# A decoder layer with routed experts: an earlier split of the routing, another order of its last logits and exponentials, and eight instead of six token tiles projected among the expert products

## The chip, the cores and the metric

The kernel runs on one core of one Trainium2 chip. The metric is the time of the whole program on the device in microseconds (us); lower is better. The engines' names are those of the profile: PE is TensorE (matrix products; PEld is its loading of weights), DVE is VectorE, ACT is ScalarE, POOL is GpSimd and SP is SyncE, which only issues DMAs in this kernel. "SPq" in a profile line is SP's DMA queue.

## The reference

One decoder layer on 16 sequences of 100 tokens, 512 wide, in float32. The part around the change is the last third:

```python
x = layernorm(x + self_attention(x))
x = layernorm(x + cross_attention(x, ctx, mask))      # ends with out @ Wo, out 2048 wide
# feed-forward: two of eight experts for each token
logits   = x @ router_w + router_b
top, idx = top_k(logits, 2)
weight   = softmax(top)
h        = silu(x @ expert_w[e] + expert_b[e])         # the reference does this for every expert e
combined = sum of weight * h[idx]
y        = x + combined @ proj_w + proj_b
x        = layernorm(x + norm_w * y / sqrt(mean(y*y) + 1e-6))
```

The kernel computes only the two chosen experts of each token.

## The kernel before

The 1600 tokens are 13 tiles of 128 (NT = 13; the last has 64). Every float32 product is made of three matmuls on PE: each operand is split (`split`, L139 to L142) into a high part, rounded to the fp32r type, and a low part, the rest, and `mm3` (L147 to L149) adds high x high, low x high and high x low. A tile of 128 x 512 times a 512 x 512 matrix is therefore 4 x 3 = 12 matmuls.

The work around the change, in its order:

1. *The output product of the cross-attention and its layer norm* (`d_part`, `d_norm`; PSUM bank `acc`; the operand halves are `ot_h`, `ot_l`). Tile after tile, each in four groups of heads; the last three tiles (TAIL = 3: 10, 11, 12) are interleaved group by group. Among them the expert weights are loaded and split into WH and WL.
2. *Router.* `d_turn(t)` transposes tile t (L985, bank `ptx`) and copies it to `x2f` (L992); `d_logits(t)` makes its 8 logits (L1004, L1008). `choose(a, b)` (L1110) takes the two largest logits of tiles a to b on DVE and ranks the tokens of each expert by small matmuls (L1149, L1160, bank `gb`).
3. *Slots.* Tokens are gathered by expert into NSL = 32 slots of 128 rows. This is done twice. `settle(0, CUT)` places the tokens of the first CUT tiles, and `slots(0, EARLY, CUT)` makes by index matmuls (L1314) the row lists of the first EARLY slots, so that these can be gathered before the last tiles are normed. `settle(CUT, NT)` and `slots(EARLY, NSL, NT)` do the rest when all tiles are routed. settle is some 40 small DVE instructions.
4. *Expert products.* For each slot i: `e_gather` (POOL, indirect DMA of rows into `xs`), `e_turn` (PE transposes into `pte`, split into `xsT`), `e_bias` (SP loads the expert's bias row `eb`), `e_product` (12 matmuls into `ph_i`), `e_out` (DVE adds the bias into `h`, L1381; ACT makes Silu of it, L1382; SP stores it to `ysd`, L1383). `h` has two buffers, `eb` three.
5. *Projection and the last norms* of a token tile: `f_gather` (POOL fetches its two rows y from ysd), `f_load` (z, which is x plus the projection's bias, and x), `f_sum` (weighted sum of the two rows), `f_turn` (transposes, bank `ptc`), `f_split`, `f_product` (12 matmuls into `pp`), then `f_square`, `f_mean`, `f_first`, `f_second` (the sums of squares, the roots, the two norms, the store of the output `out<-z`, L1694). REST tiles do this among the expert products, at the slots that the list TURN names; the rest follow after the last expert product. Tiles from LATE = 9 on gather their rows after all stores to ysd.

The weights of the two chosen experts come from the two largest logits: `ex = exp(top1 - top0)` (L1482, L1483), then 1/(1+ex). exp and Silu need different tables on ACT, so each change between them issues an ACT_TABLE_LOAD.

Each engine runs its own queue in order. Which order that is a scheduler decides when the program is built; it orders the recorded instructions by dependences and priorities: `tc.high_priority` lifts a block, `in_turn(a, b)` puts a behind b, and `tc.keep_in_program_order` fixes a DMA's place. PSUM banks are taken by name: `mm`, `s`, `t`, `av` have two each, and a bank is free for its next user when the last reader has read it. DMA issues of the hardware queues go round over eight completion counters.

Of the kernel before, what the change touches and what calls it, by code (L numbers as in the profile page):

```python
# [9 lines left out]
FP = mybir.dt.float32  # L10
FR = mybir.dt.float32r
AF = mybir.ActivationFunctionType
ALU = mybir.AluOpType
# [4 lines left out]
B, S, D = 16, 100, 512  # L18
T = B * S
KC = D // 128  # L20
# [43 lines left out]
def tile_decoder_layer(  # L64
# [29 lines left out]
    nc = tc.nc  # L94
# [3 lines left out]
    def pool(stack, name, bufs=1, **k):  # L98
        return stack.enter_context(
            tc.tile_pool(name=name, bufs=bufs, reuse_waits="tile", **k)  # L100
        )
# [6 lines left out]
    def bank(tag, shape, name):  # L108
        return ps[-1].tile(shape, FP, name=name, tag=tag)
# [12 lines left out]
    def in_turn(ins, prev):  # L122

        if prev is not None:
            tc.add_manual_dep(
                ins.ins,
                prev.ins.name,
                mybir.DependencyInfo(
                    mybir.DependencyClass.NoSync, mybir.DependencyReason.DATA
                ),  # L130
                reason="in_turn",
            )
        return ins
# [11 lines left out]
    def mm3(out, a, b, start, stop):  # L145

        nc.tensor.matmul(out, a.h, b.h, start=start, stop=False)  # L147
        nc.tensor.matmul(out, a.h, b.l, start=False, stop=False)  # L148
        nc.tensor.matmul(out, a.l, b.h, start=False, stop=stop)  # L149
# [64 lines left out]
    def kp(w):  # L214
        return w.rearrange("(k p) n -> p k n", p=128)

    NT = len(TT)
# [8 lines left out]
    w1 = pool(a_l, "a_1", 1)  # L226
# [347 lines left out]
    for k in range(KC):  # L574
        i = 4 * NU - 8 + k
# [40 lines left out]
    w1 = pool(b_l, "b_1", 1)  # L616
# [113 lines left out]
    w1 = pool(c_l, "c_1", 1, side="right")  # L730
# [134 lines left out]
    TAIL = 3  # L865
# [95 lines left out]
    gw = pool(gs, "gate", side="right")  # L961
    d_l = ExitStack()
    w1 = pool(d_l, "d_1", 1, side="right")
# [14 lines left out]
    XT2, PL = {}, {}  # L978

    def d_turn(t):  # L980
        t0, n = TT[t]
        x2 = X2.pop(t)
        pt = bank("t", [128, KC, 128], f"ptx2_{t}")
        for k in range(KC):
            nc.tensor.transpose(  # L985
                pt[:, k, :n], x2[:n, k * 128 : (k + 1) * 128], ident[:n, :n]
            )
        if t < NT - 1:
            XT2[t] = w1.tile([128, KC, 128], FP, name=f"x2f_{t}", tag="x2f")
        else:  # L990
            XT2[t] = raw[:, 0].rearrange("p (k n) -> p k n", n=128)
        nc.scalar.copy(XT2[t][:, :, :n], pt[:, :, :n])  # L992
        nc.gpsimd.tensor_tensor(x2[:n], x2[:n], pb[:n], ALU.add)
        nc.sync.dma_start(xbd[t][:n], x2[:n])
# [21 lines left out]
    URGENT = 1000  # L1016
    I32, HF = mybir.dt.int32, mybir.dt.float16
    NSL = NE + (2 * T - NE) // 128
    CUT, EARLY = NT - 4, 11

    assert EARLY <= 2 * CUT - (NE - 1)

# [39 lines left out]
    top = gw.tile([128, 2, NT], FP, name="top")  # L1062
# [243 lines left out]
    def slots(a, b, upto):  # L1306

        m = b - a
        todo = [(j, t) for t in range(upto) for j in range(2)]
        o1, o2 = 512 - 2 * m, 512 - m  # L1310
        inv, who = gb[:, o1:o2], gb[0:1, o2:]
        for dst, of in ((inv, named), (who, opens.unsqueeze(3))):
            for i, (j, t) in enumerate(todo):
                nc.tensor.matmul(  # L1314
                    dst,
                    of[:, j, t, :],
                    is_in[:, j, t, a:b],
                    start=(i == 0),
                    stop=(i == len(todo) - 1),
                )  # L1320
        idx = k1.tile([128, m], I32, name=f"idx_{a}")
        nc.vector.tensor_copy(idx, inv)
        wat = k1.tile([1, m], I32, name=f"wat_{a}")
        nc.vector.tensor_scalar(wat, who, float(KC * D), None, ALU.mult)
        bat = k1.tile([1, m], I32, name=f"bat_{a}")
        nc.vector.tensor_scalar(bat, who, float(D), None, ALU.mult)
        for i in range(a, b):
            at_ = slice(i - a, i - a + 1)
            SLOT[i] = idx[:, at_], wat[:, at_], bat[:, at_]
# [30 lines left out]
    def e_product(i, among={}):  # L1360
        xT = XS.pop(i)
        r = nc.tensor.value_load(SLOT[i][1], min_val=0, max_val=(NE - 1) * KC * D)
        ph = bank("mm", [128, D], f"ph_{i}")
        for k in range(KC):
            mm3(ph, xT[:, k, :], ew[:, bass.ds(r + k * D, D)], k == 0, k == KC - 1)
            if k in among:
                among[k]()
        PH[i] = ph

    EB = {}  # L1370
    acted = [None]

    def e_bias(i):
        rv = nc.sync.value_load(SLOT[i][2], min_val=0, max_val=(NE - 1) * D)
        EB[i] = ebb.tile([128, D], FP, name=f"eb_{i}", tag="eb", bufs=3)
        nc.sync.dma_start(EB[i], expert_b[bass.ds(rv, D)].partition_broadcast(128))

    def e_out(i):
        ph = PH.pop(i)
        h = ebb.tile([128, D], FP, name=f"h_{i}", tag="h", bufs=2)  # L1380
        nc.vector.tensor_tensor(h, ph, EB.pop(i), ALU.add)  # L1381
        acted[0] = nc.scalar.activation(h, h, AF.Silu)  # L1382
        nc.sync.dma_start(ysd[i * 128 : (i + 1) * 128, :], h)  # L1383

    early = [1, 2, 4, 5]
# [17 lines left out]
    for i in range(HEAD * NKV, len(parts)):  # L1403
        t, g = parts[i]
        if i + 1 < len(parts):
            d_load(i + 1)
        among = {}
        if t < NT - TAIL:
            if g == 1:
                d_turn(t - 1)  # L1410
            if g == 3:
                among = d_logits(t - 1)
            if g == 0 and t in (2, 4, 6, 8):
                load_expert(early[t // 2 - 1])
        elif t > NT - TAIL and g == 0:
            if t < NT - 1:
                d_turn(NT - TAIL - 1)
            else:
                among = d_logits(NT - TAIL - 1)
        elif (t, g) == (NT - 1, NKV - 1):  # L1420
            d_turn(NT - TAIL)
        d_part(i, among)
        if g == NKV - 1:
            with tc.high_priority(offset=URGENT if t >= NT - TAIL else 0):
                d_norm(t)
        if t == NT - 1 and g < NKV - 1:
            load_expert(wo_slot[g])
        if (t, g) == (CUT, 0):
            nc.sync.dma_start(raw, kp(expert_w[wo_slot[3]])[:, 2:])
        if t % 3 == 0 and t <= CUT and g == 3:  # L1430
            choose(t - 3, t)
        if (t, g) == (NT - 1, 0):
            choose(CUT, CUT + 1)
        if (t, g) == (CUT, 3):
            settle(0, CUT)
            slots(0, EARLY, CUT)
        if (t, g) == (NT - 1, 1):
            for k in range(4):
                e_gather(k)
# [11 lines left out]
    def at_once(t):  # L1451
        with tc.high_priority(offset=URGENT):
            for f in d_logits(t).values():
                f()

    e_product(1, {1: lambda: at_once(NT - 1)})
    e_turn(3)
    e_product(2, {0: lambda: at_once(NT - 2)})
    d_l.close()
    e_l = ExitStack()  # L1460
    ebb = pool(e_l, "ebb")
    for i in range(TAIL):
        e_bias(i)
    for i in range(TAIL):
        e_out(i)
    with tc.high_priority(offset=URGENT):
        choose(CUT + 1, NT)
        settle(CUT, NT)
        slots(EARLY, NSL, NT)
    slot_f = gw.tile([128, 2 * NT], FP, name="slot_f")  # L1470
    nc.vector.scalar_tensor_tensor(
        slot_f,
# [5 lines left out]
    )  # L1478
    slot = k1.tile([128, 2, NT], I32, name="slot")
    nc.vector.tensor_copy(slot.rearrange("p j t -> p (j t)"), slot_f)  # L1480
    ex = gw.tile([128, NT], FP, name="ex")
    nc.vector.tensor_tensor(ex, top[:, 1, :], top[:, 0, :], ALU.subtract)  # L1482
    nc.scalar.activation(ex, ex, AF.Exp)  # L1483
    g1 = k1.tile([128, NT], FP, name="g1")
    nc.vector.tensor_scalar(g1, ex, 1.0, None, ALU.add)
    nc.vector.reciprocal(g1, g1)
# [24 lines left out]
    F, L, C = {}, {}, {}  # L1511


    REST, LATE = 6, 9

    TURN = (19, 20, 22, 23, 25, 26, 28, 29, 31)
    BEHIND = 2

    def upto(t):
# [44 lines left out]
    def f_sum(t):  # L1564
        n = TT[t][1]
        c, y1 = F[t][0]
        ins = nc.scalar.activation(c[:n], c[:n], AF.Copy, scale=g1[:n, t : t + 1])
        tc.keep_in_program_order(in_turn(ins, acted[0]))
        nc.vector.scalar_tensor_tensor(
            c[:n], y1[:n], g2[:n, t : t + 1], c[:n], ALU.mult, ALU.add  # L1570
        )
# [45 lines left out]
    def f_mean(t):  # L1617
# [7 lines left out]
    steps = [([t, t + 1], [t - 2, t - 1] if t else []) for t in range(0, REST, 2)]  # L1625
    FIRST = len(steps)
    steps += [
        ([6], [4, 5]),
        ([7, 8], [6]),
        ([9, 10], [7, 8]),  # L1630
        ([11], [9, 10]),
        ([12], [11]),
        ([], [12]),
# [131 lines left out]
    for t in range(LATE):  # L1765
        assert TURN[t] >= upto(t)
        for lag, f in enumerate((f_fetch, f_prepare, f_project)):
            if t < REST or lag < 2:
                due.setdefault(min(TURN[t] + lag, NSL), []).append((lag, f, t))
    for i in range(FIRST):  # L1770
        due.setdefault(TURN[2 * i + 1] + 3, []).append((3, f_norm, i))
    e_bias(TAIL)
# [15 lines left out]
    for t in range(LATE, NT):  # L1788
        f_gather(t)
    done = FIRST  # L1790
    for t in range(REST + 1, LATE):
        f_load(t)
    for k in range(REST, NT + 3):
        if LATE <= k + 2 < NT:
# [90 lines left out]
```

## Time and profile before

| what | value |
|---|---|
| three runs | 1406.97, 1410.84, 1412.98 us; median 1410.84 |
| the profiled execution | 1408.13 us; span of the trace 1406.4 us |
| granted PE clock, mean over the span | 0.976 of full speed |
| busy share of the span | PE 95%, DVE 67%, ACT 54%, POOL 51% |
| output product of the cross-attention ends | 1205.4 us |
| first slots' settle on DVE | 1171 to 1198 us |
| second ranking, second settle and index matmuls | 1236.3 to 1251.2 us |
| last expert product ends | 1355.4 us |
| projections still to make after it | 8 of 13 tiles |
| last projection's last matmul ends | about 1393 us |

Times are counted from the span's start. A profile line has the start, the busy time of one entry, the engine, the source line, the operation, `out<-in` by the program's names, the shape, and in brackets how long the engine had been idle and what released it. "x3" means that three like instructions are shown as one entry. A stretch's line has its bounds, its length, and the busy time of each engine in it.

PE is the busy engine over the whole, and it runs at nearly the full clock. A full-speed matmul starts 0.23 us after the one before, at the halved clock 0.427 us.

### The profile page before, as it was taken

To read this page: it belongs to the slowest core of one execution; us is meant where nothing else is said; L and a number is where in the kernel's file an instruction comes from. 1 tells how busy PE (TensorE), PEld (TensorE's weight loads), DVE (VectorE), ACT (ScalarE), POOL (GpSimd) and SP (SyncE) were. 2 spreads that over 40 slices of the span, in tenths; PEclk is the share of its full clock that TensorE was granted. 3 is DMA by queue.
4 is the path that set the end of the run, shared out by engine and by line. 5 is a ranking of instruction groups with operands and counts; after the bars stand their busy time and mean duration, and the time that the engine had idled before them with its cause. 6 is when DMAs were issued, how large, how long until landed. Compare 5 with 4: busy or idle time off the path is not lost.

```text
span 1406.4 us, 25135 instructions
## 1 busy us (share of the span) xinstructions
PE 1331.6 (95%) x7928; PEld 1105.0 (79%) x7928; DVE 942.8 (67%) x2933; ACT 756.4 (54%) x1897; POOL 710.3 (51%) x840
## 2 busy tenths in 40 slices
PE   8999989999999999999999999999999898899894
PEld 7888868888778888888888888878887676677773
DVE  5776677776467777777777767767654558754576
ACT  4666643444446666666666666656654233333356
POOL 6878753344245555555555555545455444532530
PEclk9999989999999999999999999999999999899997
DMA  5221363544442122322233312322446545667883
GB/s 170 68 74 58 124 194 96 131 92 114 100 94 72 42 70 71 76 78 70 71 76 78 74 46 67 73 68 51 118 101 182 178 167 164 211 214 240 256 252 118
DMA packets 199160, 161.74 MB, mean 115 GB/s; under 512 B 133581, under 2 KB 153265, under 8 KB 199029
## 3 DMA queue, kind: packets, MB, share of 16 engines
q1 hardware_dynamic: 189191, 139.77, 36.2%
q0 software_dynamic: 4576, 14.95, 3.4%
q10 hardware_dynamic: 5262, 5.41, 1.3%
q8 instruction: 65, 1.06, 0.3%
q14 instruction: 66, 0.54, 0.1%
HBM read 107.25 MB, written 50.99 MB: 113 GB/s over the span
## 4 chain that ended last, share of the span: by engine, by line
PE 68%; DVE 14%; DMA 7%; ACT 4%; issue 3%; POOL 1%; SPq 1%; ACTq 1%; DVEq 0%; POOLq 0%
PE pq L147 4%; PE pq L148 4%; PE pq L149 4%; PE pv L147 4%; PE pv L148 4%; PE pv L149 4%; PE ptp L819 3%; PE pk L147 3%; PE pk L149 3%; PE pk L148 3%; PE s L147 3%; PE s L148 3%; PE s L149 3%; PE av L148 2%; PE av L147 2%
## 5 line engine op out<-in xcount | busy, mean ns | idle before, releaser
L811 POOL TENSOR_SCALAR p<-p,sums 100x361 f32<-100x361 f32 x256 | 146.4, 577 | 99.4 <-DVE sums L810 88.2
L798 DVE CUSTOM_DVE_ANT_0 p<-s,nmask 100x361 f32<-100x361 f32 x256 | 133.0, 527 | 63.4 <-PE s L149 54.7
L809 ACT ACTIVATE p<-p,nm 100x361 f32<-100x361 f32 x256 | 153.2, 601 | 39.6 <-DVE nm L798 36.3
L142 DVE TENSOR_TENSOR pT_l<-ptp,pT_h 128x400 fp32r<-128x400 f32 (+1 forms) x192 | 107.5, 568 | 57.2 <-ACT pT_h L139 56.8
L147 PE MATMUL pq<-WH 128*128 128x512 f32 (+2 forms) x272 | 107.2, 394 | 5.3 <-DVE WH L141 5.3
L819 PE MATMUL ptp<-ident,p 100*128 100x100 f32 (+1 forms) x768 | 107.4, 252 | 0.0
L139 ACT CAST pT_h<-ptp 128x400 fp32r<-128x400 f32 (+1 forms) x192 | 91.2, 487 | 30.1 <-PE ptp L819 29.7
L142 POOL TENSOR_TENSOR cT_l<-cf,cT_h 128x512 fp32r<-128x512 f32 (+1 forms) x48 | 54.4, 1133 | 103.4 <-ACT cT_h L139 101.5
L819 PEld LDWEIGHTS ptp<-ident,p 100*128 100x128 f32 (+1 forms) x768 | 95.4, 151 | 13.3 <-POOL p L811 2.3
L148 PE MATMUL pq<-WL,WH 128*128 128x512 f32 (+2 forms) x272 | 104.9, 385 | 0.0
L149 PE MATMUL pq<-WH,WL 128*128 128x512 f32 (+2 forms) x272 | 104.6, 385 | 0.0
L149 PE MATMUL acc<-WH,ot_l 128*128 128x512 f32 (+1 forms) x208 | 85.7, 413 | 7.3 <-DVE ot_l L142 5.8
L147 PE MATMUL acc<-WH,ot_h 128*128 128x512 f32 (+1 forms) x208 | 85.1, 409 | 5.0 <-ACT ot_h L139 5.0
L147 PE MATMUL s<-kT_h,WH 128*100 128x362 f32 x256 | 88.1, 355 | 0.7 <-ACT kT_h L139 0.7
L147 PE MATMUL av<-pT_h,WH 128*128 128x400 f32 (+1 forms) x192 | 76.8, 400 | 9.0 <-ACT pT_h L139 8.6
L666 POOL TENSOR_TENSOR qs<-qs,r_q 128x512 f32<-128x512 f32 (+1 forms) x52 | 54.0, 1068 | 60.9 <-DVE r_q L171 49.4
L149 PE MATMUL s<-kT_h,WL 128*100 128x362 f32 x256 | 84.3, 329 | 0.0
L148 PE MATMUL s<-kT_l,WH 128*100 128x362 f32 x256 | 83.7, 327 | 0.0
L148 PE MATMUL acc<-WL,ot_h 128*128 128x512 f32 (+1 forms) x208 | 83.6, 402 | 0.0
L142 POOL TENSOR_TENSOR WL<-qf,WH 128x400 fp32r<-128x400 f32 x64 | 67.3, 1052 | 30.5 <-ACT WH L139 26.9
L147 PE MATMUL pv<-WH,cT_h 128*128 128x512 f32 (+1 forms) x192 | 79.8, 416 | 0.9 <-DVE WL L142 0.9
L148 PE MATMUL pv<-WL,cT_h 128*128 128x512 f32 (+1 forms) x192 | 77.9, 406 | 0.0
(348 smaller groups left out, 3990.6 us busy)
## 6 DMA issues: line engine op xcount, KB each, us to landing
qf<-qd SPq DMA_DIRECT2D x64, 200.0 KB
of<-od SPq DMA_DIRECT2D x48, 256.0 KB
cf<-in_ctxT SPq DMA_DIRECT2D x16, 722.0 KB
eb<-in_expert_b SPq DMA_DIRECT2D x32, 256.0 KB
ysd<-h SPq DMA_DIRECT2D x32, 256.0 KB
f_e<-in_expert_w SPq DMA_DIRECT2D x30, 256.0 KB
f_wq<-in_Wq SPq DMA_DIRECT2D x16, 256.0 KB
f_wo<-in_Wo SPq DMA_DIRECT2D x16, 256.0 KB
```

The costliest lines, as they stand in the source:

```text
L139: ins = nc.scalar.copy(dst.h, src)
L142: low.tensor_tensor(dst.l, src, dst.h.bitcast(FP), ALU.subtract)
L147: nc.tensor.matmul(out, a.h, b.h, start=start, stop=False)
L148: nc.tensor.matmul(out, a.h, b.l, start=False, stop=False)
L149: nc.tensor.matmul(out, a.l, b.h, start=False, stop=stop)
L666: nc.gpsimd.tensor_tensor(qr[:, hs, :], qr[:, hs, :], rs[:n, hs].unsqueeze(2).to_broadcast([n, GR, HD2]), ALU.mult,)
L798: nc.vector.tensor_tensor_reduce(out=p, in0=sc[:, :SE], in1=nmask, scale=1.0, scalar=BIG, op0=ALU.add, op1=ALU.min, accum_out=nm,)
L809: nc.scalar.activation(p, p, AF.Exp, bias=nm, scale=-1.0, accum_out=sh)
L811: nc.gpsimd.tensor_scalar(p, p, sh, 1.0, ALU.mult, ALU.mult)
L819: nc.tensor.transpose(pt[:n, h, :], probs[h][:, c0 : c0 + n], ident[:S, :S])
```

## The change

It does six things.

- The first set of slots is made from tiles 0 to 7 (CUT 9 to 8) and covers 9 slots (EARLY 11 to 9). The calls of `choose` move with it: (0,3), (3,6), (6,8), then (8,10), then (10,13). Before they were (0,3), (3,6), (6,9), (9,10), (10,13).
- `x2f` has two buffers, and products 0 and 1 use bank `s` and not `mm`.
- The logits of the last two tiles, 11 and 12, are both made inside product 1; before, 12 was in product 1 and 11 in product 2.
- The last `choose`, the exponential, `settle` and `slots` are recorded ahead of the outputs of slots 0 to 2, and one Silu is put behind the exponential. The list `before_silu` ends with the exponential and is popped from its end, so that Silu is the one of slot 0; the others get nothing.
- REST is 8, not 6: tiles 6 and 7 are also projected and normed among the expert products. Their roots are taken by a Newton iteration on DVE like those of tiles 0 to 5, and not by ACT's root.
- TURN, the list of slots at which the sums and products of tiles begin, starts two slots earlier.

```diff
-            XT2[t] = w1.tile([128, KC, 128], FP, name=f"x2f_{t}", tag="x2f")
+            XT2[t] = w1.tile([128, KC, 128], FP, name=f"x2f_{t}", tag="x2f", bufs=2)
...
-    CUT, EARLY = NT - 4, 11
+    CUT, EARLY = NT - 5, 9
...
-        ph = bank("mm", [128, D], f"ph_{i}")
+        ph = bank("s" if i < 2 else "mm", [128, D], f"ph_{i}")
...
+    before_silu = [None] * NSL
...
-        acted[0] = nc.scalar.activation(h, h, AF.Silu)
+        acted[0] = in_turn(nc.scalar.activation(h, h, AF.Silu), before_silu.pop())
...
-        if (t, g) == (CUT, 0):
+        if (t, g) == (NT - TAIL - 1, 0):
             nc.sync.dma_start(raw, kp(expert_w[wo_slot[3]])[:, 2:])
-        if t % 3 == 0 and t <= CUT and g == 3:
-            choose(t - 3, t)
+        if t in (3, 6, CUT) and g == 3:
+            choose((t - 1) // 3 * 3, t)
         if (t, g) == (NT - 1, 0):
-            choose(CUT, CUT + 1)
+            choose(CUT, NT - TAIL)
...
-    e_product(1, {1: lambda: at_once(NT - 1)})
+    e_product(1, {0: lambda: at_once(NT - 2), 2: lambda: at_once(NT - 1)})
     e_turn(3)
-    e_product(2, {0: lambda: at_once(NT - 2)})
+    e_product(2)
...
+    with tc.high_priority(offset=URGENT):
+        choose(NT - TAIL, NT)
+
+        ex = gw.tile([128, NT], FP, name="ex")
+        nc.vector.tensor_tensor(ex, top[:, 1, :], top[:, 0, :], ALU.subtract)
+        before_silu.append(nc.scalar.activation(ex, ex, AF.Exp))
+        settle(CUT, NT)
+        slots(EARLY, NSL, NT)
     for i in range(TAIL):
         e_out(i)
-    with tc.high_priority(offset=URGENT):
-        choose(CUT + 1, NT)
-        settle(CUT, NT)
-        slots(EARLY, NSL, NT)
...
-    ex = gw.tile([128, NT], FP, name="ex")
-    nc.vector.tensor_tensor(ex, top[:, 1, :], top[:, 0, :], ALU.subtract)
-    nc.scalar.activation(ex, ex, AF.Exp)
...
-    REST, LATE = 6, 9
-    TURN = (19, 20, 22, 23, 25, 26, 28, 29, 31)
+    REST, LATE = 8, 9
+    TURN = (17, 18, 20, 21, 23, 24, 26, 27, 29)
...
     steps += [
-        ([6], [4, 5]),
-        ([7, 8], [6]),
-        ([9, 10], [7, 8]),
+        ([8], [6, 7]),
+        ([9, 10], [8]),
...
-    for t in range(REST + 1, LATE):
+    for t in range(LATE, REST + 2):
+        f_sum(t)
         f_load(t)
```

## The prediction

> **What bounds the kernel now.** I read the page first (TensorE, PE, is busy 95% of the span), then cut the last 235 us into stretches by the table of busy times, then went through the engines' timelines there. The change touches only the end of the last attention's output product, the expert products and the closing tail.
>
> The table of stretches (length, then busy time of each engine, granted PE clock, DMA share, GB/s):
>
> ```profile
> 1171.00:1198.00 27.00, 22.03 (x87) 15.42 (x85) 26.17 (x57) 8.48 (x16) 17.25 (x14) 0.87 0.49 151
> 1206.00:1251.00 45.00, 41.62 (x247) 33.61 (x248) 33.25 (x118) 17.46 (x32) 17.22 (x18) 0.89 0.69 219
> 1304.30:1355.40 51.10, 47.09 (x226) 38.49 (x226) 34.97 (x96) 26.15 (x53) 21.18 (x23) 0.97 0.81 255
> 1355.40:1393.10 37.70, 30.01 (x125) 21.84 (x123) 27.91 (x106) 23.31 (x52) 7.50 (x8) 0.91 0.59 182
> 1393.10:1406.40 13.30, 0.03 (x1) 0.00 (x0) 6.15 (x30) 5.97 (x14) 0.00 (x0) 0.60 0.30 109
> ```
>
> There are five limits in five stretches. In the first, DVE (VectorE) is full with settle(0,9): 26.17 of 27. From 1304 PE is the limit (47.09 of 51.1). After the last expert product (1355.4) nothing is full: PE works 30 of 37.7, and the last 13.3 us are a chain of small DVE and ACT (ScalarE) steps without PE.
>
> PE's timeline, its waits:
>
> ```profile
> 1175.85 0.44 PE L147 MATMUL acc<-WH,ot_h 128*64 128x512 f32 x1 [1.37 <-ACT ot_h L139]
> 1182.45 0.69 PE L149 MATMUL acc<-WH,ot_l 128*64 128x512 f32 x1 [3.60 <-DVE ot_l L142]
> ...
> 1259.27 1.06 PE L1356 MATMUL pte<-ident,xs 128*128 128x128 f32 x4 [0.65 <-DMA xs<-x2d,idx]
> 1260.91 0.76 PE L147 MATMUL ph<-WH,xsT_h 128*128 x1 [0.58 <-issue]
> ...
> 1368.62 0.80 PE L147 MATMUL pp<-pw_h,cp_h 128*128 128x512 f32 x1 [2.73 <-ACT pp L1600]
> ...
> 1384.66 1.01 PE L1578 MATMUL ptc<-ident,y 128*128 128x128 f32 x8 [3.02 <-DVE nm L1667]
> ```
>
> The first two are settle's bill: PE waits for halves of ot that stand behind it. The third shows that the first gathered slot, 11, costs PE almost nothing now, because products 9 and 10 ran while its rows were fetched. The last two are the tail.
>
> DVE's and POOL's timelines show why settle is slow:
>
> ```profile
> 1172.12 1.29 DVE L1094 TENSOR_SCALAR i_full<-i_full 128x8 int32<-128x8 int32 x1
> ```
>
> ```profile
> 1170.83 3.82 POOL L142 TENSOR_TENSOR WL<-f_e,WH 128x512 fp32r<-128x512 f32 x3
> ```
>
> The same L1094 takes 0.18 us at 1237.48. Here its end falls together with the first of the three splits on POOL (GpSimd), about 1.27 us each. Some ten ops of settle are drawn out so, by about 11 us of its 27.
>
> ACT's timeline around the exponential, and SP's (SyncE) queue before the last expert product:
>
> ```profile
> 1224.62 1.28 ACT L1483 ACT_TABLE_LOAD   x1
> ...
> 1230.99 1.28 ACT L1382 ACT_TABLE_LOAD   x1
> 1232.29 0.63 ACT L1382 ACTIVATE h<-h 128x512 f32<-128x512 f32 x1
> ```
>
> ```profile
> 1349.89 1.05 SPq L1694 DMA_DIRECT2D out<-z  x2
> ...
> 1354.45 0.32 SPq L1557 DMA_DIRECT2D z<-xbd  x1
> 1354.86 2.69 SPq L1383 DMA_DIRECT2D ysd<-h  x2
> ```
>
> A block of six issues (two outputs, four loads) holds SP from 1349.89 to 1354.86, 5.0 us; the stores of slots 30 and 31 are behind it.
>
> **The change, part by part.** The profiled execution took 1408.13 us, its span 1406.4; 1.7 us lie around it. The three runs' median is 1410.84, 2.7 above it. I work out a difference and put it on the median.
>
> *Early slots from eight tiles.* PE now waits 1.37 + 3.60 us, and from 1182.45 to 1187.63 it takes 12 matmuls at the halved clock: 5.18 us where 12 x 0.23 would be 2.8, so 2.4 more: 7.4 in all. In the changed order the ranking matmuls (L1149) that start settle stand 48 matmuls earlier, 48 x 0.23 = 11 us. That puts settle into 1160 to 1171, where DVE is busy 6.4 of 11 us and POOL only 2.7. DVE's total there and in the next 27 us stays the same, so the pile-up is spread over 38 us. All 7.4 can go, or none if the halves of ot are late for another reason. I take -4.5, nearer the upper end because PE stalls nowhere in 1146 to 1171.
>
> *Hand-over to the second set of slots.* Call the end of the output product Ta, 1205.4 now. The second ranking is at 1236.3 = Ta + 30.9; settle and the index matmuls end at 1251.2, 14.9 later; from there to the first gathered product (1260.91) it is 9.7 us: index casts, POOL's issue at 1252.07, a gather of 5.7, transposes, splits. After, tiles 8 and 9 are chosen during the output product and tiles 11 and 12 have their logits inside product 1: one logits wait and one ranking (about 2.6 us) less, so ranking at Ta + 28, slots at Ta + 43.2 with settle a tile wider (0.3), first gathered product at Ta + 52.9. But only nine products are early: the index matmuls stand after product 8, and the next thing on PE is the transpose of gathered slot 9. Products 9, 10, 11 then follow: one at the halved clock (1260.91 to 1266.46, 5.55), two of 2.76 and transposes of 0.44: Ta + 64.4 for the end of product 11, against 1266.6 = Ta + 61.2. So +3.2; I take +3. Bounds: -1, if the products before also shift earlier; +9, if the whole 9.7 us stand bare.
>
> *The exponential.* It is moved ahead of the Silus, but the Silu tied to it is that of slot 0 alone. ACT's order stays load, Silu(1), load, exp, load, Silu(0): three table loads as now, so nothing is saved. New is that store 0 waits for exp. Exp now ends at 1227.75 = Ta + 22.3; load 1.28 and Silu 0.63 give Ta + 24.2; a store has landed at most 3.4 us after issue (issued 1232.94, its buffer rewritten at 1236.30): Ta + 27.6. Slot 3's bias add, which needs that buffer, comes at 1233.09 = Ta + 27.7. By the row the cost is 0. The Trainium skill, "ScalarE: Activation LUTs", section "What ACT_TABLE_LOAD costs", counts a drain of about 1.38 us on top of each load; that would put the store at Ta + 29.0 and stop DVE for 1.3 us, with the second ranking's result queued behind. In this trace Silu runs at 1232.29, 0.02 us after the load's end, so I take 0 and keep 1.3 for the range. That slots 0 and 1 use other PSUM banks frees two banks for products 2 and 3, which no row shows waiting: 0.
>
> *Two more projections among the products.* Each is 12 matmuls x 0.23 = 2.72 on PE and a transpose of 0.44. PE is 92% busy from 1304 to 1355, so they lie on the path: 2 x 3.16 = +6.3; 5.4 if they fill part of PE's idle 4 us. Their DVE work (3.5 us each) and ACT's have room: 34.97 and 26.15 of 51.1. Their loads of x and z (tiles 7 and 8) move from ACT's queue to SP's.
>
> *The tail.* From product 31's end to the end of the span it is 51.0 us: eight projections in 37.7, 4.7 each, then 13.3. Two fewer: -9.4. The floor comes from the last gathers: POOL issues the last at 1365.01, by the gather time of 5.7 it lands at 1371; tile 12's sum, transpose, split and product need some 6 us, then 13.3: end at 1390, 35 us after 1355.4. So -9.4 fits above the floor; -14 if the loads also cease to stall (2.73 at 1368.62), -2 if they stall more.
>
> Sum: -4.5 + 3.0 + 0 + 6.3 - 9.4 = -4.6. On the profile 1403.5, on the median **1406.2**.
>
> **Rivals.**
>
> *Faster: settle's stall is gone and the tail runs freely.* -7.4 + 2 + 6.3 - 12.5 = -11.6, 1399. For it: the free DVE and POOL time in 1160 to 1171, and the 5.8 us of PE waits in the tail. Against: DVE is needed 27.9 of 37.7 there, and the gathers keep their time.
>
> *Slower: SP's queue.* In the changed order one block of outputs and four loads (5.0 us) stands ahead of the stores of slots 28 to 30, and a second one ahead of store 31. A block waits for norms that are now made among the products. h has two buffers, so a late store stops a bias add on DVE, then a PSUM bank, then PE; store 31 also releases the last gathers. If both blocks stand bare, 2 x 5.0, and the 2.73 stall for a late load comes once more: -4.6 + 10 + 2.7 = +8.1, 1419. It decides when store 28 goes out more than about 3 us late: two buffers give two products of 3.2 us, 6.4, less 3.4 for a store to land. For it: now there is one such block, and the z load issued at 1354.45 is used only at 1367.06. Against: before the first block PE shows no wait for it now.
>
> *The hand-over is bare.* +9 in place of +3, and 1.3 for the table load: +2.7, 1413.5.
>
> *The change only moves work.* Settle's stall stays, the tail gains what the products lose, the exponential's order saves nothing, the hand-over is even: 0, 1411.
>
> **How the numbers follow.** My forecast 0.38, its own range 1401 to 1411 (0.14 of it below 1403.8); faster rival 0.26; SP's queue 0.22 (all above 1417.9); hand-over 0.10 (0.05 above); work only moved 0.04. A measurement of this kernel tells about 0.5%, 7 us, from no change. Faster by more: 0.14 + 0.26 = 0.40. Slower by more: 0.22 + 0.05 = 0.27. Within: 0.33. The range 1397 to 1420 leaves out the outer part of the faster rival and of SP's, about 0.1 each.
>
> **What would show it.** Right: PE's two waits for ot under 2 us together; the first gathered slot's transpose waiting some 5 us or more for its gather; three table loads still; seven projections before product 31's end; the stretch from there to the end 40 to 43 us. Wrong: stores 28 to 31 issued late with PE waiting for bank ph before 1355; a tail above 47 us; or waits for ot that remain.

## The result

The changed kernel is slower. Its four runs have a median of 1428.3 us (1425.96 to 1431.07) beside 1411.91 for the kernel before: ratio 1.0118, 95% interval 1.0079 to 1.0156. Measured once more with another set of runs it was 1422.56 to 1409.86, ratio 1.0080 (1.0046 to 1.0115). The prediction was 1406.2, range 1397 to 1420.

**How the two traces are compared.** The spans differ by 17.9 us (1424.3 and 1406.4), but 9.6 of these lie ahead of the first router transpose (1072.9 before, 1082.5 after), where both kernels issue the same instructions in the same order. In the sixteen traces of this study that transpose stands anywhere from 1068.0 to 1082.5, also for kernels that are alike up to there. So I count from it. One stage of one trace is not exact either: the output product took 131.6, 132.8, 134.8 and 136.6 us in four kernels that do it alike, a spread of 5 us.

| us | output product | to end of product 11 | products 12 to 31 | tail | sum |
|---|---|---|---|---|---|
| before | 132.8 | 61.0 | 88.9 | 50.9 | 333.6 |
| changed | 135.0 | 67.6 | 93.0 | 46.1 | 341.7 |
| changed, second trace | 137.2 | 68.8 | 93.2 | 45.9 | 345.0 |
| predicted difference | -4.5 | +3.0 | +6.3 | -9.4 | -4.6 |
| measured difference | +2.2, +4.4 | +6.6, +7.8 | +4.1, +4.3 | -4.8, -5.0 | +8.1, +11.5 |

(The first column runs from the first router transpose to the output product's end, the tail from the end of product 31.) The sum, 8.1 to 11.5 us, is 0.6 to 0.8% of the time and fits the second ratio.

The runs below give more traces that are alike in a stage. The output product took 131.6 to 136.6 us in the four with the order of before (mean 133.9) and 134.7 to 137.4 in the five with the changed order (136.1). To the end of product 11 it was 60.8 to 62.5 in four against 67.6 to 68.8 in four, so this difference is clear. Products 12 to 31 took 85.9 to 88.9 in five that order them as before (87.2) and 93.0 to 96.1 in seven that order them as the change (94.1), which is +6.9.

The table of stretches of the changed kernel (length, then PE, PEld, DVE, ACT, POOL busy, granted clock, DMA share, GB/s): first settle, end of output product to index matmuls, first projection to product 31, rest of the projections, end.

```profile
1166.30:1191.20 24.90, 18.15 (x74) 12.26 (x74) 22.56 (x63) 6.67 (x13) 10.41 (x8) 0.91 0.37 115
1217.50:1264.80 47.30, 40.09 (x236) 32.59 (x234) 31.47 (x106) 17.43 (x32) 16.63 (x16) 0.86 0.60 189
1318.90:1378.10 59.20, 59.20 (x290) 49.05 (x291) 44.22 (x126) 31.82 (x63) 22.47 (x23) 0.97 0.75 243
1378.10:1406.80 28.70, 23.23 (x93) 16.15 (x91) 18.66 (x66) 15.64 (x35) 7.72 (x8) 0.88 0.61 209
1406.80:1424.30 17.50, 0.02 (x1) 0.00 (x0) 9.12 (x51) 9.70 (x23) 0.00 (x0) 0.56 0.26 97
```

From 1318.9 to 1378.1 PE is never idle. The loss lies ahead of that stretch and in the products, and the gain behind it is half of what was counted on. PE's waits of the changed kernel:

```profile
1188.95 0.69 PE L149 MATMUL acc<-WH,ot_l 128*64 128x512 f32 x1 [6.46 <-DVE ot_l L142]
...
1222.34 1.11 PE L1356 MATMUL pte<-ident,xs 128*128 128x128 f32 x4 [3.92 <-ACT x2f L992]
...
1249.18 0.76 PE L147 MATMUL ph<-WH,xsT_h 128*128 x1 [2.86 <-DVE rank L1167]
...
1270.47 1.08 PE L1356 MATMUL pte<-ident,xs 128*128 128x128 f32 x4 [5.53 <-DMA xs<-x2d,idx]
...
1388.27 1.03 PE L1581 MATMUL ptc<-ident,y 128*128 128x128 f32 x4 [3.10 <-DVE y L1572]
```

The first is one long wait in the output product where before had two (1.37 and 3.60). The next three are new at this length: before the first expert product (0.61 before), before product 5 (none), and before the first gathered slot (0.65), 12.3 us together. The transposes of slots 0 to 8 end, the next rows are not there, and nothing else is left for PE to do: before, products 9 and 10 ran there.

The first wait on DVE's and POOL's timelines:

```profile
1178.52 1.53 DVE L183 TENSOR_SCALAR x<-x,mv_ln,r_ln 128x512 f32<-128x512 f32 x1
1179.98 1.31 DVE L1264 SCALAR_TENSOR_TENSOR new<-first,new 128x64 f32<-128x64 f32 x1
1181.21 1.33 DVE L1268 SCALAR_TENSOR_TENSOR fills<-first,fills 128x64 f32<-128x64 f32 x1
1182.58 1.19 DVE L1271 TENSOR_TENSOR first<-first,new 128x64 f32<-128x64 f32 x1
...
1188.48 0.42 DVE L142 TENSOR_TENSOR ot_l<-of,ot_h 128x256 fp32r<-128x256 f32 x1
```

```profile
1178.47 3.99 POOL L142 TENSOR_TENSOR WL<-f_e,WH 128x512 fp32r<-128x512 f32 x3 [4.79 <-ACT WH L139]
1182.42 1.27 POOL L142 TENSOR_TENSOR ot_l<-of,ot_h 128x512 fp32r<-128x512 f32 x1
1183.64 1.27 POOL L993 TENSOR_TENSOR x<-x,pb 128x512 f32<-128x512 f32 x1
1184.86 1.27 POOL L142 TENSOR_TENSOR WL<-f_e,WH 128x512 fp32r<-128x512 f32 x1
```

settle did start earlier, by the 48 matmuls that were counted: 265 matmuls of the output product stand ahead of its ranking for 313 before. Nearly all of its first 30 instructions were quick. Then six instructions of POOL, four of them splits, ran back to back from 1178.47 to 1186.1, and six instructions of DVE in a row ahead of the half tile's ot_l took 1.2 to 1.5 us each, one to each instruction of POOL. PE waited for exactly that ot_l.

This does not by itself make the stage longer than before, where settle stretched in the same way. PE's idle time in the whole stage is 13.9 us (15.1 in the second trace) and was 13.4; its busy time is 121.1 and was 119.4:

```profile
1082.50:1217.60 135.10, 121.06 (x589) 92.10 (x587) 85.05 (x258) 40.91 (x86) 68.99 (x62) 0.96 0.54 172
1072.90:1205.70 132.80, 119.42 (x583) 91.77 (x581) 85.94 (x248) 42.50 (x89) 67.33 (x61) 0.96 0.55 175
```

(The first line is the changed kernel.) What can be said is that the waits for ot stayed: in the last 40 us of the stage they are 6.9 to 7.8 us in five traces of the changed order and 5.0 to 7.8 in the four of the order before.

ACT around the exponential, SP ahead of the store, and DVE behind it:

```profile
1236.26 1.28 ACT L1471 ACT_TABLE_LOAD   x1
1238.86 0.21 ACT L1471 ACTIVATE ex<-ex 128x13 f32<-128x13 f32 x1 [1.32 <-DVE ex L1470]
1239.09 1.28 ACT L1384 ACT_TABLE_LOAD   x1
1240.39 0.63 ACT L1384 ACTIVATE h<-h 128x512 f32<-128x512 f32 x1
```

```profile
1239.76 2.28 SPq L1560 DMA_DIRECT2D z<-xbd  x5
1242.22 0.34 SPq L1378 DMA_DIRECT2D eb<-in_expert_b  x1
1242.66 0.85 SPq L1385 DMA_DIRECT2D ysd<-h  x2
```

```profile
1248.34 0.69 DVE L1383 TENSOR_TENSOR h<-ph,eb 128x512 f32<-128x512 f32 x1 [4.42 <-DMA ysd<-h]
1248.95 0.17 DVE L1167 COPY rank<-gb 128x24 f32<-128x24 f32 x1
```

Slot 0's Silu runs at 1240.39, its store is issued at 1242.66 behind five z loads, and slot 3's bias add gets the buffer at 1248.34, 5.7 us later (6.8 in the second trace). The second ranking was ready on PE at 1245.8; DVE takes it up at 1248.95.

### The profile page after: what moved, and what is told of

It reads as the page before. It is cut to its first block, busy times and chain, and to the rows that moved or that the text cites. A ratio compares the mean times of both kernels' runs of the same rounds, so it can differ in the third digit from the quotient of the medians.

```text
span 1424.3 us, 25134 instructions
## 1 busy us (share of the span) xinstructions
PE 1333.7 (94%) x7924; PEld 1103.9 (78%) x7924; DVE 938.1 (66%) x2940; ACT 756.3 (53%) x1896; POOL 714.9 (50%) x840
## 4 chain that ended last, share of the span: by engine, by line
PE 61%; DVE 14%; DMA 12%; ACT 6%; issue 4%; POOL 1%; SPq 1%; ACTq 0%; DVEq 0%; POOLq 0%
PE pv L147 4%; PE pv L148 3%; PE pv L149 3%; PE ptp L819 3%; PE pk L147 3%; PE pk L149 3%; PE pk L148 3%; PE s L147 3%; DMA qd<-qTb 3%; PE s L149 3%; PE s L148 3%; PE pq L147 2%; PE pq L149 2%; PE pq L148 2%; PE av L148 2%
## 5 line engine op out<-in xcount | busy, mean ns | idle before, releaser
L147 PE MATMUL av<-pT_h,WH 128*128 128x400 f32 (+1 forms) x192 | 76.6, 399 | 13.9 <-ACT pT_h L139 13.5
L666 POOL TENSOR_TENSOR qs<-qs,r_q 128x512 f32<-128x512 f32 (+1 forms) x52 | 54.0, 1069 | 58.4 <-DVE r_q L171 47.4
L147 PE MATMUL pk<-WH,cT_h 128*128 128x512 f32 (+1 forms) x192 | 78.1, 407 | 0.3
```

What stands on the lines that cost most here:

```text
L666: nc.gpsimd.tensor_tensor(qr[:, hs, :], qr[:, hs, :], rs[:n, hs].unsqueeze(2).to_broadcast([n, GR, HD2]), ALU.mult,)
```

## The experiments

Theory A was, from the traces: the loss is made of separate waits (ot behind a settle that POOL stretches; the buffer of slot 0 behind exponential and SP queue; the bare gather), and the projections are near even. Rivals are in each expectation. Stages of one trace each, as in the table above, and the ratio to before with its interval:

| us | output product | to end of 11 | 12 to 31 | tail | sum | ratio |
|---|---|---|---|---|---|---|
| proj_only | 131.6 | 60.8 | 88.7 | 55.6 | 336.7 | 1.0040 (1.0023 to 1.0057) |
| dense_turn | 136.6 | 62.3 | 90.2 | 55.9 | 345.0 | 1.0062 (1.0043 to 1.0082) |
| routing_only | 137.4 | 68.2 | 89.3 | 50.8 | 345.7 | 1.0052 (1.0039 to 1.0065) |
| free_silu | 134.7 | 65.9 | 95.8 | 45.6 | 342.0 | 1.0055 (1.0036 to 1.0074) |
| cut9 | 134.1 | 69.7 | 96.1 | 44.4 | 344.3 | 1.0050 (1.0035 to 1.0065) |
| merged_steps | 136.2 | 67.8 | 93.1 | 44.1 | 341.2 | 1.0086 (1.0059 to 1.0113) |
| splits_on_dve | 128.0 | 65.0 | 86.6 | 46.6 | 326.2 | 0.9985 (0.9970 to 1.0000) |
| one_expert_dve | 137.7 | 61.7 | 87.9 | 49.8 | 337.1 | 1.0014 (0.9995 to 1.0032) |
| after_splits | 130.5 | 71.5 | 93.0 | 42.9 | 337.9 | 1.0040 (1.0026 to 1.0054) |
| after_mended | 132.7 | 62.8 | 94.2 | 43.7 | 333.4 | 1.0002 (0.9982 to 1.0021) |
| before_merged | 134.8 | 62.5 | 85.9 | 47.0 | 330.2 | 0.9990 (0.9969 to 1.0011) |
| mended_z_late | 133.0 | 57.6 | 96.2 | 41.8 | 328.6 | 0.9991 (0.9978 to 1.0003) |
| before_both | 130.2 | 66.9 | 86.8 | 46.9 | 330.8 | 0.9987 (0.9972 to 1.0002) |

### Is the 1.2% the change's?

No edit: the changed kernel as it is.

> The changed kernel unaltered, beside the kernel before on one chip. In the first profiles, before and after differ by 17.9 us of span, of which 9.6 lie ahead of the first router transpose, where the order of the instructions is the same. Theory A (those 9.6 are drift between executions; the change costs +2 in the output product, +7 at the hand-over, +4 in the products, -4.6 in the tail): ratio 1.005 to 1.008. Rival (the change slows the early part too): 1.011 to 1.013, and the first router transpose again about 1082.

Ratio 1.0080 (1.0046 to 1.0115), at the upper end of theory A's figure; the first router transpose stood at 1080.6. Both traces of the change have it late, but so has splits_on_dve (1080.6), which is the kernel before up to there, and merged_steps, which is the change up to the tail, has it at 1074.1. So most of the 9.6 us is drift between executions; that a small part of it belongs to the change can't be excluded.

### The projections alone

```diff
-    REST, LATE = 6, 9
+    REST, LATE = 8, 9
...
-        ([6], [4, 5]),
-        ([7, 8], [6]),
-        ([9, 10], [7, 8]),
+        ([8], [6, 7]),
+        ([9, 10], [8]),
```

(with the loop after it as in the change, in the kernel before)

> The kernel before with the projections' part of the change alone: REST 8, the steps and the loop after it as in the change; CUT 9, EARLY 11 and TURN as before (TURN cannot start earlier while EARLY is 11). Theory A (the loss is in routing and its hand-over; the projections are near even): from the end of the output product to the end of product 31 some 4 to 6 us longer than before's 150.0, from there to the end some 4 to 5 shorter than 51.0, total within 2 us of before, ratio 0.999 to 1.002. Rival B (the projections are what costs): slower by 8 us or more, ratio 1.006 or above. The first router transpose, before which the change moves nothing, stands at 1072.9 in the profile of before and at 1082.5 in that of the change: if that is drift between executions it lies anywhere between these here; if it belongs to the routing part it is at 1073.

Slower by 0.4%, between A and B, and not by A's way: the products are as before, and the tail is 4.8 us longer, not shorter. With TURN as it was, only five projections start before product 31 ends, as before, and what is left of the edit is its queue: the loads of tiles 7 and 8 stand on SP behind outputs that wait for norms, where before they were on ACT's queue; DVE waits 3.19 us for a z there. That is the queue that the prediction's slow rival named, in another place. The next run shows it plainly.

```diff
-    TURN = (19, 20, 22, 23, 25, 26, 28, 29, 31)
+    TURN = (19, 20, 21, 23, 24, 25, 27, 28, 29)
```

(on top of proj_only)

> The kernel before with REST 8 and a denser TURN (19, 20, 21, 23, 24, 25, 27, 28, 29) in place of an earlier one, so that EARLY stays 11 and the hand-over as before. Theory A (the projections' part pays only if it comes without the smaller first set of slots): hand-over as before (product 11 ends 61 after the output product), products 3 to 5 us longer than before, tail 3 to 5 shorter than in the run with the projections alone (55.6); ratio 0.999 to 1.003. Rival (eight tiles among the products cost more than they save wherever they stand): 1.005 or above.

1.0062, the rival's side. In dense_turn DVE's timeline has

```profile
1383.99 1.40 DVE L1598 TENSOR_TENSOR z<-pp,z 128x512 f32<-128x512 f32 x2 [8.57 <-DMA z<-xbd]
```

and PE stands 15.2 us up to 1393.2. So eight tiles cost time here. To get their projections in earlier takes the earlier TURN, and that takes the smaller EARLY: the kernel's own assertion wants TURN at EARLY + 8 or later. The two halves of the change are tied. That eight tiles pay even with the earlier TURN isn't shown: products and tail together take 139.1 us in both traces of the changed kernel and 139.8, 137.7 and 133.2 in three kernels with the order of before (before, one_expert_dve, splits_on_dve), where the prediction had a gain of 3.1.

### The routing alone

The change with REST, the steps, the loop and TURN put back.

> The changed kernel with REST 6, its steps and TURN as before: everything of the change but the projections. Theory A: the two waits for ot on DVE and ACT together over 5 us as in the change, first gathered product some 55 us after the end of the output product and a bare gather wait of about 5 us; 8 to 10 us slower than before, ratio 1.006 to 1.007, and 1.012 if the 9 us ahead of the first router transpose belong to it too. Rival B: ratio below 1.003.

1.0052, near A. The output product with 137.4, the first gathered wait of 5.70 and product 11 at 68.2 are the change's; the tail is that of before. So routing and hand-over cost about 7 us by the ratio, and nothing in that part pays them back.

### Slot 0's Silu

```diff
-        acted[0] = in_turn(nc.scalar.activation(h, h, AF.Silu), before_silu.pop())
+        acted[0] = nc.scalar.activation(h, h, AF.Silu)
```

> The changed kernel without the edge that puts slot 0's Silu behind the exponential; Silu of slots 0 and 1 then stand ahead of the exponential on ACT, as before. Theory A (store 0 is late behind the exponential and five z loads, DVE waits 4.42 us for its buffer with the second ranking's result behind it): that wait goes under 1 us, PE's wait of 2.86 us before product 5 goes, the index matmuls end about 3 us earlier after the end of the output product (44 instead of 47.3); ratio about 1.009 to before, 3 us better than the change. Rival: the store would be late anyway because of SP's queue, nothing moves, 1.012.

Half right. PE's wait before product 5 is gone (one of 2.10 us before the index matmuls is left), and the index matmuls end at 45.5 after the output product (47.4 and 48.3 in the change); product 11 ends 1.7 us earlier. But DVE's wait did not go under 1 us: a store is now awaited for 6.37 us, by the bias add of another slot, with the second ranking behind it as before. So the exponential was not the only thing ahead of the stores. In this one trace what was won here went again in products 12 to 31 (95.8): ahead of the first projection's transposes PE waits 3.06 us, 2.10 in the change. The single ratio, 1.0055, is below that of the change, with intervals that overlap.

### Where settle stands

```diff
-    CUT, EARLY = NT - 5, 9
+    CUT, EARLY = NT - 4, 9
```

> The changed kernel with CUT 9 and EARLY 9: the first slots are settled after tile 8 as in the kernel before, but only nine of them. Theory A (settle at its earlier place collides with the expert splits on POOL, and the last half tile's low part stands behind it on DVE): PE's waits for ot together are back near before's 5 us or below, where the change has 7.6; the bare gather wait of 5.5 us stays. Ratio 1.008 to 1.011. Rival (the waits for ot are due to late loads of the attention output, whatever settle does): waits of 7 us or more stay.

The waits for ot did not tell the two apart (9.25 us from the first router transpose on, 9.33 in the change, 10.94 before), so A's place for settle is not shown by this run. It does show two other things. The bare gather wait stays (4.93), with nine early slots whatever CUT is. And the wait for x2f before the first expert product is gone (first product 3.5 us after the output product, 7.3 and 7.0 in the two traces of the changed kernel).

### Is it POOL that stretches settle?

```diff
-    def load_expert(e, last=False):
+    def load_expert(e, last=False, low=None):
...
-                nc.vector if last and k else nc.gpsimd,
+                nc.vector if last and k else low or nc.gpsimd,
...
-            load_expert(wo_slot[g])
+            load_expert(wo_slot[g], low=nc.vector)
```

In the kernel before:

> The kernel before with the low parts of the three experts loaded during the last tile's output product (12 splits) made on DVE and not on POOL. Theory A (settle is slow because its two-input instructions wait for POOL's splits): settle's small instructions stay at about 0.2 us where some ten of them now take 1.0 to 1.4, and the first settle, 27 us now, takes under 22 although DVE gets splits of 0.7 us in it; PE's waits for ot together change by less than 3 us. Total within 3 us of before. Rival (the long instructions are long by themselves or by a wait for something else): they stay at 1.0 to 1.4 us.

The instructions are quick now; the same lines as in the change's fence:

```profile
1194.07 0.23 DVE L1264 SCALAR_TENSOR_TENSOR new<-first,new 128x72 f32<-128x72 f32 x1
1194.22 0.23 DVE L1268 SCALAR_TENSOR_TENSOR fills<-first,fills 128x72 f32<-128x72 f32 x1
1194.48 0.23 DVE L1271 TENSOR_TENSOR first<-first,new 128x72 f32<-128x72 f32 x1
```

With POOL's splits away 0.23, with them 1.2 to 1.3. The Trainium skill, "SBUF — State Buffer", section "Who interferes with whom", states that an instruction of DVE with two inputs in SBUF contends with one of POOL that reads SBUF; here the price is about 1 us each time. Instructions with one input are stretched too: L1094, 1.29 us in the kernel before, takes 0.16 here. The total gain is small (0.9985) because DVE, with twelve splits more, finishes settle later and the first expert product starts 13.2 us after the output product, not 3.2. In the changed kernel:

> The changed kernel with the low parts of the last three experts' weights split on DVE and not on POOL. Theory A (in the change, seven instructions of settle and of a layer norm are stretched from 0.2 to some 1.2 us at 1178 to 1186 by POOL's splits, and the last half tile's low part stands behind them): PE's longest wait for ot_l, 6.46 us, goes below 3, the settle instructions stay near 0.2 us, and the output product takes 3 to 5 us less from the first router transpose (135 to 137 now). The transposes of tile 10 and of the first slot then wait less than 3.9 us for ACT if that wait is a follow of the stall. Rival (late loads of the attention output): the wait stays above 5 us.

The long wait for ot is gone: 4.24 us in all from the first router transpose, for 9.3 to 9.8, and the output product is 4.5 to 6.7 us shorter. The same lines once more, this time in the same kernel as the change's fence but for the splits, with what POOL still does:

```profile
1173.72 0.22 DVE L1264 SCALAR_TENSOR_TENSOR new<-first,new 128x64 f32<-128x64 f32 x1
1175.19 0.22 DVE L1271 TENSOR_TENSOR first<-first,new 128x64 f32<-128x64 f32 x1
1175.44 1.18 DVE L1272 TENSOR_TENSOR first<-first,fills 128x64 f32<-128x64 f32 x1
1176.66 1.21 DVE L1273 TENSOR_TENSOR new<-first,new 128x64 f32<-128x64 f32 x1
```

```profile
1174.59 1.95 POOL L142 TENSOR_TENSOR ot_l<-of,ot_h 128x512 fp32r<-128x512 f32 x1 [6.63 <-ACT ot_h L139]
1176.51 1.28 POOL L993 TENSOR_TENSOR x<-x,pb 128x512 f32<-128x512 f32 x1
```

Two instructions are still long, and they stand beside the two that POOL has left there. So the cause is shown: it is POOL's two-input work, whichever it is.

The wait for x2f has gone with it (first product at 3.6). In the changed kernel the copy to x2f stands on ACT behind casts of expert weights, and these were late:

```profile
1210.07 0.62 ACT L139 CAST ot_h<-of 128x512 fp32r<-128x512 f32 x1 [6.11 <-DMA of<-od]
1216.22 0.62 ACT L139 CAST WH<-f_e 128x512 fp32r<-128x512 f32 x1 [3.32 <-DMA f_e<-in_expert_w]
1219.96 0.62 ACT L139 CAST WH<-f_e 128x512 fp32r<-128x512 f32 x1 [3.13 <-DMA f_e<-in_expert_w]
```

The last two loads of these weights were issued within 0.6 us of the output product's end; in the kernel before the last one went out 7.2 us ahead of it. POOL's splits and the earlier settle together make this so: with either away (after_splits, cut9) the first product is on time. The wait for ot is not what makes it late, for cut9 has the same waits. How the loads fall behind is not shown step by step.

Here, too, DVE pays later: index matmuls at 51.0, product 11 at 71.5. With one expert only on DVE:

```diff
+            load_expert(wo_slot[g], low=None if g else nc.vector)
```

> The kernel before with only the first of the three last experts split on DVE (the one whose splits fall in settle). With all three there, the output product was 4.8 us shorter but the first expert product came 10 us later because settle's end was late. Theory A: most of the 4.8 stays and the first product comes as in before, ratio 0.995 to 0.999. Rival (the gain is only moved): 0.999 to 1.002.

In the kernel before this does nothing (1.0014): the output product is not shorter. In the changed kernel, where that one expert's splits meet settle, it was run only together with two other edits (below).

### The end of the tail

```diff
-        ([11], [9, 10]),
-        ([12], [11]),
-        ([], [12]),
+        ([11, 12], [9, 10]),
+        ([], [11, 12]),
```

> The changed kernel with the norm steps of tiles 11 and 12 taken as one ([11, 12] with the second norms of 9 and 10, then the second norms of 11 and 12): one root fewer at the end. Theory A (after product 12 the end is a chain of root, first norm, square, next root, some 3.6 us a step, four of them in the change where before has three): the stretch from the last matmul to the end goes from 17.5 to about 14, ratio 2 to 3 thousandths below that of the unaltered change. Rival (the end waits for tile 12's own work): the stretch stays above 16.5.

The stretch after the last matmul went from 17.5 to 16.1, not to 14: the chain of roots is part of it, but most of what it has over the 13.3 of before stayed. The ratio does not resolve it. In the kernel before:

> The kernel before with the norm steps of tiles 11 and 12 as one. In the change this took 1.4 us off the stretch after the last matmul, where 3.5 were expected. If the chain of roots sets the end here too: 13.3 goes to about 12 and the ratio is 0.998 to 1.000; if tile 12's own work sets it: no change.

12.5 for 13.3, ratio 0.999, within noise.

### All together

One expert's splits on DVE, the free Silu and the merged step, in the changed kernel:

> The changed kernel with three edits at once: the first of the last three experts split on DVE, slot 0's Silu free, and the norm steps of tiles 11 and 12 as one. If the three losses are separate: output product -3, index matmuls -2.5, end chain -1.5, that is about 7 of the 11 us lost: ratio 1.001 to 1.004. If a later limit (the bare gather, the last gathers) takes them back: 1.006 or above.

1.0002 (0.9982 to 1.0021): the loss is gone, and the stages show it at the three places (132.7, 62.8 and 43.7 for 135.0, 67.6 and 46.1). How much each of the edits gives in company isn't separated. Waits for ot 3.26 us in all, first expert product at 1.7, index matmuls at 41.7, product 11 at 62.8. The bare gather stays:

```profile
1253.73 1.08 PE L1356 MATMUL pte<-ident,xs 128*128 128x128 f32 x4 [5.17 <-DMA xs<-x2d,idx]
```

The last open wait, for a store, by the z loads ahead of it:

```diff
-        nc.sync.dma_start(ysd[i * 128 : (i + 1) * 128, :], h)
+        stored[0] = nc.sync.dma_start(ysd[i * 128 : (i + 1) * 128, :], h)
...
-                nc.sync.dma_start(dst[:n], src[:n])
+                in_turn(nc.sync.dma_start(dst[:n], src[:n]), stored[0])
```

> The changed kernel with the three mends of the run before (one expert's splits on DVE, slot 0's Silu free, tiles 11 and 12 in one norm step) and a fourth: each z load of tiles 0 to 8 is put behind the last store to ysd recorded before it, so that five of them no longer stand ahead of the stores of slots 2 and 3 on SP. There, DVE still waits 3.82 us for a store before the second ranking is taken up. Theory A (that wait is the five z loads'): it goes below 1 us, the index matmuls end 2 us earlier (39 to 40 after the output product for 41.7), the ratio is 0.998 to 1.000. Rival (the wait is the store's own time to land): it stays above 3 us and the ratio at 1.000 or above.

```profile
1228.94 0.69 DVE L1383 TENSOR_TENSOR h<-ph,eb 128x512 f32<-128x512 f32 x1 [2.46 <-DMA ysd<-h]
1229.55 0.17 DVE L1167 COPY rank<-gb 128x24 f32<-128x24 f32 x1
```

In between: the wait is 2.46 for 3.82. From its issue the awaited store took 4.0 us to release the buffer (1224.97 to 1228.94), and 5.3 in the run before, behind the five loads (1230.48 to 1235.81). So some of it was the z loads and some is the store's own way. The index matmuls end 4.5 us earlier (37.2, further than expected), product 11 at 57.6; the products then give 2 us back. Ratio 0.9991 (0.9978 to 1.0003). The kernel before with the mends that fit it:

> The kernel before with the two mends that can be made there: the last three experts' low parts split on DVE (0.9985 alone) and tiles 11 and 12 in one norm step (0.999 alone). If these are separate gains: ratio 0.996 to 0.999; if the tail absorbs the one: 0.9985 to 1.000.

0.9987 (0.9972 to 1.0002). None of the versions is faster than the kernel before beyond doubt.

## Why the prediction was wrong

Three terms failed: the output product in kind, and the hand-over and the tail in size.

**The output product (-4.5, measured +2.2 and +4.4): the step that failed in kind.** The prediction saw that POOL stretches settle, and reckoned that an earlier settle would meet an idle POOL, "so the pile-up is spread over 38 us". It looked at how busy POOL was on average in 1160 to 1171. settle did not end there: it ran to 1191, and its second half met six instructions of POOL back to back, four of them splits. Also the cost is not settle's length but which instruction stands behind it: DVE works in order, and the half tile's ot_l stood last. The two waits that were to go, 1.37 + 3.60, became one of 6.46 (5.92 in the second trace). One of the two was misread besides. The half of ot that PE waited 1.37 us for is ACT's and stood behind a cast that waited for its load, not behind settle:

```profile
1174.87 0.62 ACT L139 CAST WH<-f_e 128x512 fp32r<-128x512 f32 x1 [3.34 <-DMA f_e<-in_expert_w]
1175.39 0.40 ACT L139 CAST ot_h<-of 128x256 fp32r<-128x256 f32 x1
```

That the gain failed to come is clear. That the stage became longer is not: +2.2 between the means lies within the spread of 5 us, and PE's idle time in it grew by 0.5 and 1.7 us only.

**The hand-over (+3.0, measured +6.6 and +7.8): mechanism right, one term missing.** Counted from the end of the output product, the second ranking came at 28.3 (28 was worked out), in spite of a first expert product 4 us late, which the prediction had not in it. The gather lay bare, as said: 5.5 us. What failed is the step from the ranking to the index matmuls' end, 47.4 and 48.3 instead of 43.2. The ranking lay 3.1 and 4.1 us until DVE took it up, because a bias add ahead of it waited for the store of slot 0. For that store I took "a store has landed at most 3.4 us after issue" from one row of a quiet moment, and cost 0. It took 5.7 and 6.8, and issue itself came behind five z loads on SP that the prediction, which named SP's queue elsewhere, did not count here. Two smaller errors nearly cancel: the first gathered product came 7.3 us after the index matmuls and not 9.7, and products 9 to 11 took 12.9 and not 11.5. The table load behaved as the row said and not as with the drain: Silu follows the load's end by 0.02 us again (1239.09 + 1.28 to 1240.39).

**The exponential's order saves nothing: right.** Three table loads, as before.

**The products (+6.3, measured +4.1 and +4.3, or +6.9 between the means): right.** PE was the limit, and from 1318.9 on it is busy without a gap; the prediction's own lower figure was 5.4. (12 x 0.23 is 2.76 and not 2.72, so the sum should have read 6.4.)

**The tail (-9.4, measured -4.8 and -5.0): wrong in its last term.** The share of 4.7 us for each projection held: from product 31 to the last matmul it is 28.7 us (28.5) where before had 37.6, so -8.9. What failed is that the end behind it was carried over as 13.3. It took 17.5, and 17.4 to 17.7 in all five traces that have the change's norm steps and its TURN. When the last matmul ends, four roots are still to be taken on ACT (at 1407.30, 1412.16, 1415.78 and 1418.66) where before had three: one more norm step is left when the products are done sooner. Taking one step out (merged_steps) gave back 1.4 us; where the rest comes from stays open. The floor of 35 us missed the same term, and put tile 12's way from its rows to its product at 6 us where it took about 12 (last gather issued at 1388.59, 5.7 to land, last matmul's end at 1406.8), with DVE 15.2 of 19.4 us busy from 1387.4 to there.

**The rivals.** That the hand-over is bare was the nearest: 1413.5 was said, +2.7, and with the measured +2.2 or +4.4 in place of its -4.5 it would have said +9.4 or +11.6, close to the measured +8.1 and +11.5. That is luck in part, since its hand-over was some 3 us too large and its tail 4.5 too good. SP's queue did not decide in the changed kernel: the block of loads does stand ahead of the stores of slots 28 to 30, and PE shows no wait there. It decided in the two runs with the projections alone, as a late z.

## What to carry to other kernels

Before moving a chain of small instructions on an in-order engine to a quieter place, follow it to its end: look at what the other engine does while the last of the chain runs, and at what stands behind the last. When a batch is made smaller so that it can start sooner, ask what work had covered the latency of the next batch. And when work ahead of a program's closing chain gets shorter, work out the length of that chain anew: what had been done beside the work that went may be left for the end.

## What the runs showed of the hardware

A two-input DVE instruction of 0.23 us took 1.2 to 1.3 while POOL ran two-input instructions of 1.27 us back to back, one DVE instruction for each POOL instruction, and 0.23 in splits_on_dve, where POOL was idle beside it. From issue until its buffer could be written again, a store of 128 x 512 floats took at most 3.4 us in a quiet moment of the kernel before, 4.0 in mended_z_late with no z loads ahead of it, and 5.3 to 7.8 with five loads ahead of it (four traces). From the index matmuls' end to the first product from gathered rows it was 6.9 to 7.5 us in seven of the nine traces with nine early slots, 5.1 to 5.7 of it a wait of PE for the gather. And the first 1070 us of one instruction order differed by 14 us between executions, more than the whole effect in question.
